# One ReLU of the next pair placed ahead of the next block's exponential on ScalarE (two adaLN layers: RWKV with experts, then pairwise attention with a ternary feed-forward)

## The chip, the core and the metric

The kernel runs on one core of a Trainium2 chip. A core has four compute engines that take their instructions in order, each from its own queue: TensorE (PE in the profile; its weight loads are listed as PEld), VectorE (DVE), ScalarE (ACT) and GpSimd (POOL). SyncE (SP) issues transfers. Engines wait for each other through semaphores. The metric is the device time of one launch in microseconds: the median of several runs, without a profiler.

## The reference

Two layers act on x of 4 batches x 1024 tokens x 256 channels, in float32. Each has an attention branch and a feed-forward branch, both behind a layer norm that is scaled and shifted per batch, and both added to x through a gate per channel. The first layer is an RWKV recurrence and a mixture of 8 experts. The second layer, where the change acts, has pairwise attention and a ternary feed-forward:

```python
q = einsum('bnc,ac->bna', X, Wq)            # a = 64
k = einsum('bnc,ac->bna', X, Wk)
Vy = einsum('bnc,dc->bnd', X, Wy_w) + Wy_b
e = relu(signed_sqrt(q[:, :, None, :] + k[:, None, :, :]))   # sqrt(relu(x)+1e-8) - sqrt(relu(-x)+1e-8)
scores = einsum('bija,a->bij', e, Wphi)
ex = exp(scores - max_j scores)
part1 = einsum('bij,bjc->bic', ex, Vy)
Ew = einsum('bij,bija->bia', ex, e)
part2 = einsum('bia,ca->bic', Ew, We_w) + We_b * denom
(part1 + part2) / (denom + 1e-9)

h = silu(x @ w1 * s1) * (x @ w2 * s2)       # 256 -> 1024
h = gelu(h @ h1 * s3); h = gelu(h @ h2 * s4)
y = h @ w3 * s5                             # 1024 -> 256
```

The array e has 4 x 1024 x 1024 x 64 elements, 268 million. Each one takes an add, a ReLU, a square root, a part in the scores and a part in Ew.

## The kernel before

The program runs the first layer in `first_layer`, up to about 1230 us, but leaves the experts of its last batch over. Then `pair_attention` (line 829 on) runs the second layer, with the left-over experts as the first task beside it, to about 4930 us. The last feed-forward tasks follow.

**Blocks, pairs, halves.** The queries are cut into 128 blocks of 32, 32 blocks to a batch. A block's work on e has 16 halves. Half i holds 16 queries x 8 channels on the 128 partitions and the 1024 keys along the free dimension: 16 queries by `i // 8`, the channel group by `i % 8`. Two halves make a pair, so a block has pairs p = 0 to 7; a pair lives in one slot, a tile of 128 x 2 x 1024, of a ring of 14 slots (`RING`).

**What is done to a half.** `kB[i % 8]` holds the keys of one channel group, repeated over the queries. One instruction adds the half's query (one number per partition) and takes the maximum with zero. Which engine does this is fixed by i: GpSimd for `ADD_ON_POOL` = 1, 3, 5, 9, 11, 13 (line 1387), ScalarE, as a ReLU with a bias, for `RELU_ON_SCALAR` = 2, 6, 8, 12, 14 (line 1409), VectorE for 0, 4, 7, 10, 15 (line 1398). ScalarE then takes the square root of the whole pair (line 1410), and TensorE multiplies it by the weights of the scores into the PSUM tile `sc` (line 1414, eight matmuls per pair).

**The softmax.** When all eight pairs are in, `top` takes the maximum over the keys on VectorE (lines 1424 and 1426) and brings the quarters together on TensorE (1427). `exps` forms `neg`, the negative maximum (VectorE, 1431), and the exponential (ScalarE, 1433). Behind the exponential, `switch` issues a SiLU or GELU of the feed-forward task if one is queued (1363). The square root, the exponential and the GELU or SiLU each have another activation table, so `ACT_TABLE_LOAD` instructions stand between them.

**The second use of e.** `spread` copies the exponentials to all partitions with matmuls against `pick` (`xb`, line 1440); `weigh` multiplies a half by `xb` in place and sums over the keys into a column of `ew` (VectorE, line 1460). `turn` and `turned` transpose the exponentials (1447, 1451). Every fourth block `finish` makes the attention's output from them: copies of `ew` (1480), matmuls into `o` (1511, 1523), the division (1530 to 1533) and the addition to x on GpSimd (1535). Every eighth block a feed-forward task `dense` of 256 tokens is added: matmuls at 1251, 1321 and 1342, their scaling on VectorE at 1286, 1305 and 1352.

**The order.** The scheduler leaves the order as it is written (`manual_schedule`); the loop at the end of `pair_attention` writes it. For block n it goes through p = 0 to 7. Each step weighs both halves of pair p of block n (with VectorE's adds for the next pair to be made between the two), puts in pieces of the tasks (`work`, with a budget per step, `ROOM`), and then begins and makes one pair of a later block:

```python
while begun <= 8 * n + p + ahead[0]:
    begin()
    make()
```

`begin` takes a slot and issues GpSimd's adds of a new pair; `make` runs `pair` (VectorE's adds if not yet done, ScalarE's ReLUs, the square root, the score matmuls) for the pair that was begun two calls earlier (`LEAD`). `ahead` is 13 while the left-over experts run, about the first 12 blocks, and 14 from then on. At p = 5 the loop calls `top` of block n + 1, at p = 6 `exps` and the first `spread` of block n + 1. With `ahead` = 14, pair 1 of block n + 2 has been made just before that exponential, and pairs 2 and 3 have been begun but not made.

**Slots.** A pair's slot comes free when its second half has been weighed. Which free slot a new pair gets is settled by the order in which the program first writes to the new tiles.

Of the kernel before, what the change touches and what calls it, by code (L numbers as in the profile page):

```python
# [8 lines left out]
AF = mybir.ActivationFunctionType  # L9
# [35 lines left out]
def block_kernel(ctx: ExitStack, tc: tile.TileContext, a, out):  # L45
# [26 lines left out]
    nc.gpsimd.memset(seen, 0.0)  # L72
    first_layer(tc, a, link, cols, seen, ident, eps)
    pair_attention(tc, a, link, out, cols, seen, ident, eps)


# [753 lines left out]
def pair_attention(tc, a, link, out, cols_of, seen, ident, eps):  # L830
# [10 lines left out]
    nc = tc.nc  # L841
    NB = T // 32
# [3 lines left out]
    with tc.tile_pool(name="at_k", bufs=1) as pk, tc.tile_pool(name="at_w", bufs=1) as wp, tc.tile_pool(  # L846
# [14 lines left out]
        kB, qtab, kds, vds = {0: {}}, {0: link["qt"][0]}, {0: link["kd"]}, {0: link["vd"]}  # L861
# [17 lines left out]
        for i in range(2):  # L879
            t = wp.tile([P, 4, P], F32, tag=f"ewt{i}", name=f"ewt{i}")  # L880
            nc.gpsimd.memset(t, 0.0)
            ewt.append(t)
            t = wp.tile([P, 4, 64], F32, tag=f"ew{i}", name=f"ew{i}")
# [379 lines left out]
        def follower():  # L1263

            return groups.get(stream[1]) if len(stream) > 1 else None
# [103 lines left out]
        class Block:  # L1369


            def __init__(self, n):
                self.n, self.b, self.s, self.added = n, n // NB, {}, set()
                self.sc = psc.tile([P, 512], F32, tag="sc", name="sc")

            def on_scalar(self, i):
# [5 lines left out]
            def begin(self, p):  # L1382
                self.s[p] = ring.tile([P, 2, T], F32, tag="s", name="s")
                for h in range(2):
                    i = 2 * p + h
                    if self.n and i in ADD_ON_POOL:
                        nc.gpsimd.tensor_scalar(  # L1387
                            self.s[p][:, h, :], kB[self.b][i % 8], self.query(i), 0.0, ALU.add, ALU.max
                        )

            def adds(self, p):
# [3 lines left out]
                for h in range(2):  # L1395
                    i = 2 * p + h
                    if not (self.n and i in ADD_ON_POOL or self.on_scalar(i)):
                        nc.vector.tensor_scalar(  # L1398
                            self.s[p][:, h, :], kB[self.b][i % 8], self.query(i), 0.0, ALU.add, ALU.max
                        )  # L1400

            def pair(self, p):
                t = self.s[p]
                s = p // 4
                self.adds(p)
                for h in range(2):
                    i = 2 * p + h
                    if self.on_scalar(i):
                        nc.scalar.activation(t[:, h, :], kB[self.b][i % 8], AF.Relu, bias=self.query(i))  # L1409
                nc.scalar.activation(t, t, AF.Sqrt, bias=eps_rho)  # L1410
                for h in range(2):
                    g = (2 * p + h) % 8
                    for j in range(4):
                        nc.tensor.matmul(  # L1414
                            self.sc[32 * j : 32 * j + 32, 0:256],
                            wsel[:, g, 16 * (1 - s) : 16 * (1 - s) + 32],
                            t[:, h, 256 * j : 256 * (j + 1)],
                            start=p == 0 and h == 0,
                            stop=p == 7 and h == 1,
                        )  # L1420
# [121 lines left out]
        N = B * NB  # L1542
        blocks = {0: Block(0)}
        begun = made = 0
# [3 lines left out]
        def work(room):  # L1548


            tick()
            turns[0] += 1
            if issues and turns[0] % 2:
                issues.pop(0)()
            for of in (tasks, stream):
                while of and room > 0:
                    got = next(of[0], self_done)
                    if got is self_done:
                        of.pop(0)
                    elif got is None:  # L1560
                        break
                    else:
                        room -= got
# [10 lines left out]
        def make():  # L1574
            nonlocal made
            n, p = made // 8, made % 8
            if n < N:
                blocks[n].pair(p)
                if n % NB == NB - 1 and n + 1 < N and p >= 4:
                    for g in range(2 * p - 8, 2 * p - 6):  # L1580
                        spread_keys(n // NB + 1, g)
            made += 1
# [13 lines left out]
        for n in range(N):  # L1596
            cur = blocks.pop(n)
            ew = ews[n // 4 % 2]
            if n % 4 == 0:
                exT = p2.tile([P, 4, 2, P], F32, tag="exT", name="exT")  # L1600
            nxt = n + 1 < N
            if n % NB == PREP and n // NB + 1 < B:
                stream.insert(min(1 + (follower() in heads), len(stream)), prepare(n // NB + 1))
            for p in range(8):
                if p == 0:
                    cur.spread(1)
                    cur.turn()
                if p == 2:
                    cur.turned(exT)
                cur.weigh(p, 0, ew)  # L1610
                if made < 8 * N:
                    blocks[made // 8].adds(made % 8)
                cur.weigh(p, 1, ew)
                if nxt and p == 5:
                    blocks[n + 1].top()
                if nxt and p == 6:
                    blocks[n + 1].exps()
                    blocks[n + 1].spread(0)
                work(ROOM[p])
# [3 lines that stand above are left out]
            if n % 4 == 3:  # L1623
                tasks.append(finish(n, ew, exT))
# [104 lines left out]
```

## Time and profile before

| | us |
|---|---|
| runs without a profiler | 5089.64, 5089.88, 5096.81; median 5089.88 |
| the profiled execution | 5104.67, its span 5102.4 |
| PE, DVE, ACT, POOL busy | 4335.7, 4171.3, 3691.2, 3401.3 |
| mean granted TensorE clock | 0.90 of full speed |

| row | count | mean ns |
|---|---|---|
| square root of a pair, L1410 | 1024 | 2000 |
| ReLU of a half on ScalarE, L1409 | 641 | 1138 |
| add of a half on VectorE, L1398 | 645 | 914 |
| add of a half on GpSimd, L1387 | 762 | 3798 |
| weighing of a half, L1460 | 2048 | 1210 |
| exponential, L1433 | 128 | 474 |
| its table load, L1433 | 128 | 1283 |

In a row of a group, the numbers after the count are the busy time in all, the mean of one in ns, and then the time for which the engine sat idle just before such instructions, with the line that ended most of it. In a row of a timeline the first two numbers are the start and the length in us, and square brackets give the idle time just before the instruction and what released it. Rows of a timeline can hold several instructions (x3). Times on GpSimd are rough.

### The profile page before, as it was taken

The page shows a single profiled execution, that of the slowest core. Times are in us where ns is not written, and L with a number is a line of the kernel's source. Part 1 is how long each engine was busy: PE and PEld are TensorE (multiplying, and loading weights), DVE is VectorE, ACT ScalarE, POOL GpSimd, SP SyncE. Part 2 cuts the span into 40 slices and gives each one's busy share as a digit, 9 for nine tenths or more (in the row PEclk, how much of TensorE's full clock was granted, in tenths as well). Part 3 has the DMA queues.
Part 4 walks back from the last instruction along what each step waited for, and adds up shares of the span by engine and source line. Part 5 has one row for each costly group of instructions (what it writes and reads, how often), then busy time and mean ns, then how long its engine had stood idle before and what let it go on. Part 6 is the DMA issues. An engine that isn't in the chain of part 4 may idle for free.

```text
span 5102.4 us, 75603 instructions
## 1 busy us (share of the span) xinstructions
PE 4335.7 (85%) x28714; PEld 2442.9 (48%) x28714; DVE 4171.3 (82%) x7255; ACT 3691.2 (72%) x3438; POOL 3401.3 (67%) x1231
## 2 busy tenths in 40 slices
PE   6788888878688879888897989888889889798888
PEld 2233333333344545555554555555455556455557
DVE  4877777776889888889888888888888988988871
ACT  2322322225888898999998989999888999999961
POOL 3433434334678778788877778787877877887840
PEclk7798988889788999999898999999889989999999
DMA  4333333343012222222121323222123322122223
GB/s 136 83 101 110 95 93 92 93 118 119 27 33 71 80 82 91 101 78 69 57 85 47 121 76 110 70 70 84 60 83 103 103 70 84 60 79 67 75 80 114
DMA packets 255946, 429.41 MB, mean 84 GB/s; under 512 B 71784, under 2 KB 142624, under 8 KB 255328
## 3 DMA queue, kind: packets, MB, share of 16 engines
q1 hardware_dynamic: 252512, 422.09, 26.5%
q8 instruction: 226, 3.70, 0.3%
q10 hardware_dynamic: 2880, 1.98, 0.1%
q14 instruction: 136, 1.11, 0.1%
q0 software_dynamic: 192, 0.52, 0.0%
HBM read 400.32 MB, written 40.93 MB: 86 GB/s over the span
## 4 chain that ended last, share of the span: by engine, by line
PE 35%; ACT 18%; DVE 15%; issue 7%; POOL 1%; DMA 0%; ACTq 0%; POOLq 0%; SPq 0%; DVEq 0%
PE ff_ps L1321 14%; PE sc L1414 10%; DVE s L1460 9%; ACT s L1410 9%; ACT s L1409 4%; PE xb L1440 3%; DVE s L1398 2%; PE out_ps L1342 2%; PE o L1511 2%; ACT L1410 2%; ACT L1363 1%; PE o L1523 1%; ACT wide L1363 1%; PE ff_ps L1251 1%; ACT ex L1433 1%
## 5 line engine op out<-in xcount | busy, mean ns | idle before, releaser
L1387 POOL TENSOR_SCALAR s<-kB,qt 128x1024 f32<-128x1024 f32 x762 | 2883.6, 3798 | 600.7 <-DVE ew L1460 476.4
L1460 DVE CUSTOM_DVE_ANT_0 s<-s,xb 128x1024 f32<-128x1024 f32 x2048 | 2418.3, 1210 | 36.2 <-PE xb L1440 35.0
L1410 ACT ACTIVATE s<-s,eps 128x2048 f32<-128x2048 f32 x1024 | 2027.2, 2000 | 76.1 <-DVE s L1398 29.8
L1414 PE MATMUL sc<-s,wsel 128*32 128x256 f32 x16384 | 1194.8, 416 | 398.9 <-ACT s L1410 396.8
L1321 PE MATMUL ff_ps<-wide,fw 128*128 128x256 f32 x4096 | 1007.5, 395 | 29.3 <-ACT wide L1363 25.7
L1414 PEld LDWEIGHTS sc<-s,wsel 128*32 128x32 f32 x16384 | 456.2, 115 | 997.7 <-ACT s L1410 590.1
L1321 PEld LDWEIGHTS ff_ps<-wide,fw 128*128 128x128 f32 x4096 | 766.9, 195 | 238.1 <-issue 99.4
L1409 ACT ACTIVATE s<-kB,qt 128x1024 f32<-128x1024 f32 x641 | 729.0, 1138 | 17.9 <-DVE acc L594 16.6
L1398 DVE TENSOR_SCALAR s<-kB,qt 128x1024 f32<-128x1024 f32 x645 | 588.9, 914 | 0.9 <-DMA same<-in_same_dram 0.9
L736 POOL TENSOR_TENSOR kv<-vb,out_k 128x512 f32<-128x512 f32 x256 | 324.1, 1274 | 279.1 <-DVE state L804 196.8
L611 PE MATMUL e_ps<-wd,hid 128*128 128x512 f32 x896 | 427.8, 625 | 0.4 <-DVE acc L594 0.4
L1440 PE MATMUL xb<-ex,pick 64*128 64x256 f32 x2048 | 328.8, 445 | 57.0 <-ACT ex L1433 57.0
L804 DVE TENSOR_TENSOR_SCAN state<-dec,carry,kv 128x512 f32<-128x512 f32 x256 | 325.9, 1273 | 10.8 <-ACT dec L791 10.7
L611 PEld LDWEIGHTS e_ps<-wd,hid 128*128 128x128 f32 x896 | 175.6, 202 | 249.0 <-issue 242.3
L1440 PEld LDWEIGHTS xb<-ex,pick 64*128 64x128 f32 x2048 | 197.7, 209 | 196.4 <-ACT ex L1433 97.7
L1251 PE MATMUL ff_ps<-wide,fw 128*128 128x256 f32 x1024 | 265.4, 408 | 6.1 <-ACT wide L935 5.8
L806 DVE TENSOR_TENSOR pr<-state,rec 128x512 f32<-128x512 f32 x256 | 176.0, 688 | 87.6 <-ACT state L802 34.4
L796 ACT COPY carry<-state 128x1 f32<-128x1 f32 x255 | 47.9, 188 | 269.6 <-DVE state L804 268.2
L1251 PEld LDWEIGHTS ff_ps<-wide,fw 128*128 128x128 f32 x1024 | 197.2, 201 | 65.3 <-issue 26.6
L1424 DVE TENSOR_REDUCE sc<-sc 128x1 f32<-128x256 f32 x128 | 54.9, 429 | 210.0 <-PE sc L1414 210.0
L1305 DVE TENSOR_TENSOR wide<-ff_ps,ffn_s 128x512 f32<-128x512 f32 x128 | 87.8, 686 | 168.0 <-PE ff_ps L1321 168.0
L1433 ACT ACTIVATE ex<-sc,neg 128x256 f32<-128x256 f32 x128 | 60.7, 474 | 199.9 <-DVE neg L1431 198.9
(252 smaller groups left out, 4006.6 us busy)
## 6 DMA issues: line engine op xcount, KB each, us to landing
fw<-in_ffw_dram SPq DMA_DIRECT2D x354, 512.0 KB
vb<-vd SPq DMA_DIRECT2D x1024, 64.0 KB
lent<-vd SPq DMA_DIRECT2D x64, 514.0 KB
wd<-in_w_down_dram SPq DMA_DIRECT2D x28, 1024.0 KB
kB<-kd SPq DMA_DIRECT2D x32, 512.0 KB
lent<-in_We_dram SPq DMA_DIRECT2D x32, 512.0 KB
kd<-nd SPq DMA_DIRECT2D x24, 512.0 KB
vd<-out_v SPq DMA_DIRECT2D x8, 512.0 KB
```

What stands on the lines that cost most here:

```text
L611: nc.tensor.matmul(ps, hid[:, k, t * P : (t + 1) * P], wd[:, k, :], start=k == 0, stop=k == HID // P - 1)
L736: nc.gpsimd.tensor_mul(kv, vb[:, g % 2, :], ready[u]["k"][:, n // HN, :])
L804: nc.vector.tensor_tensor_scan(s[:, 1 : U + 1], dec, kv, c, ALU.mult, ALU.add)
L1251: nc.tensor.matmul(ps[:, h, :], w[:, k, o : o + P], hT[:, k, :], start=k == 0, stop=k == 1)
L1321: nc.tensor.matmul(ps[:, h, :], w[:, k * P : (k + 1) * P], of[:, k, :], start=k == 0, stop=k == 7)
L1387: nc.gpsimd.tensor_scalar(self.s[p][:, h, :], kB[self.b][i % 8], self.query(i), 0.0, ALU.add, ALU.max)
L1398: nc.vector.tensor_scalar(self.s[p][:, h, :], kB[self.b][i % 8], self.query(i), 0.0, ALU.add, ALU.max)
L1409: nc.scalar.activation(t[:, h, :], kB[self.b][i % 8], AF.Relu, bias=self.query(i))
L1410: nc.scalar.activation(t, t, AF.Sqrt, bias=eps_rho)
L1414: nc.tensor.matmul(self.sc[32 * j : 32 * j + 32, 0:256], wsel[:, g, 16 * (1 - s) : 16 * (1 - s) + 32], t[:, h, 256 * j : 256 * (j + 1)], s ...
L1440: nc.tensor.matmul(xb[:, 256 * j : 256 * (j + 1)], pick[q, j % 2, s, :], self.ex[q, :], start=True, stop=True)
L1460: nc.vector.tensor_tensor_reduce(t[:, h, :], t[:, h, :], self.xb[s], 1.0, 0.0, ALU.mult, ALU.add, ew[:, self.n % 4, col : col + 1])
```

## The change

ScalarE's ReLUs of a pair get a function of their own, `relus`, which `pair` calls where the code stood before and which does nothing the second time. At p = 6 the loop calls it, ahead of `exps`, for the pairs that have been begun but not yet made.

```diff
             def __init__(self, n):
-                self.n, self.b, self.s, self.added = n, n // NB, {}, set()
+                self.n, self.b, self.s, self.added, self.relued = n, n // NB, {}, set(), set()
...
+            def relus(self, p):
+                if p in self.relued:
+                    return
+                self.relued.add(p)
+                for h in range(2):
+                    i = 2 * p + h
+                    if self.on_scalar(i):
+                        nc.scalar.activation(self.s[p][:, h, :], kB[self.b][i % 8], AF.Relu, bias=self.query(i))
+
             def pair(self, p):
                 t = self.s[p]
                 s = p // 4
                 self.adds(p)
-                for h in range(2):
-                    i = 2 * p + h
-                    if self.on_scalar(i):
-                        nc.scalar.activation(t[:, h, :], kB[self.b][i % 8], AF.Relu, bias=self.query(i))
+                self.relus(p)
                 nc.scalar.activation(t, t, AF.Sqrt, bias=eps_rho)
...
                 if nxt and p == 6:
+                    for m in range(made, min(begun, 8 * N)):
+                        blocks[m // 8].relus(m % 8)
                     blocks[n + 1].exps()
                     blocks[n + 1].spread(0)
```

With `ahead` = 14 the pairs are 2 and 3 of block n + 2. Pair 2 (halves 4 and 5) has no half on ScalarE, pair 3 has half 6. With `ahead` = 13 they are pairs 1 and 2, and the half is number 2. So one ReLU of 128 x 1024 goes ahead of each of 126 of the 128 exponentials. On ScalarE it is moved past the exponential with its table load, the queued SiLU or GELU with its load, the load back to the square root's table, and, with `ahead` = 14, the square root of pair 2. The orders on the other engines' queues are unchanged, and no transfer is issued at another place. The slot of pair 3 is now first written at this ReLU, so pair 3 gets the slot of the current block's pair 5, where it had that of pair 6; pair 4, whose first write is GpSimd's add of half 9, gets the slot of pair 6 where it had that of pair 5.

## The prediction, made before the changed kernel was run

> **What bounds the kernel now.** I read the page's engine totals first, then its costliest groups, then the busy time of the pair-attention stage (1230 to 4930 us), where the change acts, and last the timelines of ScalarE, TensorE, VectorE and GpSimd over one stretch of eight blocks (4228 to 4455 us).
>
> ```profile
> PE 4335.7 (85%) x28714; PEld 2442.9 (48%) x28714; DVE 4171.3 (82%) x7255; ACT 3691.2 (72%) x3438; POOL 3401.3 (67%) x1231
> ```
>
> ```profile
> 1230.00:4930.00 3700.00, 3168.53 (x25276) 1915.49 (x25277) 3219.28 (x5739) 3337.77 (x2506) 2918.72 (x814) 0.91 0.23 75
> ```
>
> The columns of the second are window, length, then PE, PE loads, DVE, ACT, POOL. Over the whole run ScalarE looks idle for a quarter; inside the stage it is the fullest engine: 3337.8 of 3700 is 90%, beside 87% for VectorE and 86% for TensorE. It idles for 362 us there, and the groups say where:
>
> ```profile
> L1387 POOL TENSOR_SCALAR s<-kB,qt 128x1024 f32<-128x1024 f32 x762 | 2883.6, 3798 | 600.7 <-DVE ew L1460 476.4
> ...
> L1410 ACT ACTIVATE s<-s,eps 128x2048 f32<-128x2048 f32 x1024 | 2027.2, 2000 | 76.1 <-DVE s L1398 29.8
> ...
> L1409 ACT ACTIVATE s<-kB,qt 128x1024 f32<-128x1024 f32 x641 | 729.0, 1138 | 17.9 <-DVE acc L594 16.6
> L1398 DVE TENSOR_SCALAR s<-kB,qt 128x1024 f32<-128x1024 f32 x645 | 588.9, 914 | 0.9 <-DMA same<-in_same_dram 0.9
> ...
> L1424 DVE TENSOR_REDUCE sc<-sc 128x1 f32<-128x256 f32 x128 | 54.9, 429 | 210.0 <-PE sc L1414 210.0
> ...
> L1433 ACT ACTIVATE ex<-sc,neg 128x256 f32<-128x256 f32 x128 | 60.7, 474 | 199.9 <-DVE neg L1431 198.9
> ```
>
> 199 us of ScalarE's idle time lie ahead of the exponential, which waits for VectorE's maximum, which waits (210 us) for the last score matmuls. That is the pocket that the change puts a ReLU of 1.138 us into. But the pocket is uneven. Listing the idle time ahead of each of 127 exponentials: 53 have 1.13 us or more, 48 have under 0.05, the rest lie between. Cut off at 1.134 us each, the pockets hold 74.7 us: that is all that can be filled. In the other direction the exponentials become late by 127 x 1.134 - 74.7 = 69 us in sum. Neither sum is a time yet: what counts is which wait ends last next.
>
> Two exponentials, one with a pocket and one without:
>
> ```profile
> 4252.03 1.28 ACT L1433 ACT_TABLE_LOAD   x1
> 4257.26 0.47 ACT L1433 ACTIVATE ex<-sc,neg 128x256 f32<-128x256 f32 x1 [3.95 <-DVE neg L1431]
> 4257.75 1.28 ACT L1410 ACT_TABLE_LOAD   x1
> 4259.05 2.00 ACT L1410 ACTIVATE s<-s,eps 128x2048 f32<-128x2048 f32 x1
> 4260.95 1.13 ACT L1409 ACTIVATE s<-kB,qt 128x1024 f32<-128x1024 f32 x1
> ```
>
> ```profile
> 4424.31 0.47 ACT L1433 ACTIVATE ex<-sc,neg 128x256 f32<-128x256 f32 x1
> 4424.81 1.28 ACT L1363 ACT_TABLE_LOAD   x1
> 4426.10 2.00 ACT L1363 ACTIVATE wide<-wide 128x1024 f32<-128x1024 f32 x2
> 4428.12 1.28 ACT L1410 ACT_TABLE_LOAD   x1
> 4429.41 2.00 ACT L1410 ACTIVATE s<-s,eps 128x2048 f32<-128x2048 f32 x1
> 4431.32 1.13 ACT L1409 ACTIVATE s<-kB,qt 128x1024 f32<-128x1024 f32 x1
> ```
>
> In both, the last row is the ReLU that moves up, in front of the exponential's table load. In the first it costs nothing and ScalarE is 1.13 us ahead from then on; in the second the exponential, the GELU behind it and the next square root all come 1.13 us later.
>
> **The change part by part.** Nothing is added or removed. One ReLU (pair 3, half 6) per block moves past the exponential's load (1.28), the exponential (0.47), the stream's activation where there is one, the load back (1.28) and the square root of pair 2 (2.00). TensorE's, VectorE's, GpSimd's and SyncE's own orders stay; no DMA is issued at another place. The number of table loads stays too, since ReLU runs between two square roots today without one.
>
> *What the moved ReLU waits for.* Its slot must be free: it takes the slot of the current block's pair 5, whose last weighing is ahead of the maximum on VectorE, so this wait has ended before any exponential can run. At the three changes of batch it also waits for a load of `kB`, now ahead of an exponential: 3 times; bounds 0 and some 5 us in all (the group's whole wait on that load was 0.7 us), taken as 0.
>
> *ScalarE, over the eight blocks from 4228.6 to 4454.5*, a pattern that returns nine times (idle ahead of the exponentials 2.06, 3.95, 0.47, 0, 4.36, 0, 0, 0):
> 1. 4228.6, idle 2.06: hidden. The 1.13 us lead dies at the next exponential, which waits 3.95 us for TensorE's side. 0.
> 2. 4257.3, idle 3.95: hidden; the lead dies at a square root that waits 1.05 us for a VectorE add. 0.
> 3. 4283.6, idle 0.47: exponential and GELU 0.67 late; TensorE has a wait of 0.72 ahead where it regains this. 0.
> 4. 4313.0, no idle: 0.67 late (it starts with a lead of 0.47), but TensorE isn't waiting for it. 0.
> 5. 4342.5, idle 4.36: hidden, a lead of 1.13.
> 6. 4367.2, no idle: the lead pays for the ReLU, GELU on time. 0; the new lead dies at two waits for the stream's layer norm (0.47 and 1.18).
> 7. 4398.1, no idle: 1.13 late; TensorE and VectorE have made it up by 4413. 0.
> 8. 4424.3, no idle: 1.13 late, and this one lies on the path:
>
> ```profile
> 4431.47 1.07 PE L1414 MATMUL sc<-s,wsel 128*32 128x256 f32 x16 [2.65 <-ACT s L1410]
> ```
>
> ```profile
> 4441.74 0.87 DVE L1286 SCALAR_TENSOR_TENSOR wide<-ff_ps,ffn_s,wide 128x256 f32<-128x256 f32 x2 [3.24 <-PE ff_ps L1251]
> ```
>
> TensorE waits for that square root, then goes through the FFN matmuls that VectorE waits for, and the maximum at 4454.5 comes some 1.06 us later. Sum of a period: +1.06.
>
> *Slots.* The ring gives a slot to whoever writes it first in the program. The ReLU now takes pair 5's slot, so GpSimd's first add of pair 4 (half 9) must wait for pair 6's second weighing; in the trace it starts 1.7 to 7.1 us ahead of that weighing's end. GpSimd then starts the next adds up to 0.67 us later; it waits 476 us for VectorE in 204 places, and pair 4's square root comes some 8 us after that weighing with the add done at 3.9. Cost 0; without that cover it would be 0.67 per block.
>
> *VectorE beside GpSimd.* Some VectorE adds are stretched while GpSimd adds:
>
> ```profile
> 4339.63 1.60 DVE L1398 TENSOR_SCALAR s<-kB,qt 128x1024 f32<-128x1024 f32 x1
> ```
>
> ```profile
> 4329.63 11.05 POOL L1387 TENSOR_SCALAR s<-kB,qt 128x1024 f32<-128x1024 f32 x3
> ```
>
> ```profile
> 4436.63 0.74 DVE L1398 TENSOR_SCALAR s<-kB,qt 128x1024 f32<-128x1024 f32 x1
> ```
>
> The first add, 2.6 us into GpSimd's third operation, took 1.60 us; the last, 2.1 us into one too (GpSimd ran three from 4426.80), took 0.74. The stretched add sits directly ahead of the maximum of step 5, and GpSimd's half 9 would no longer be there: -0.85 per period. In exchange the add after the maximum (half 7) comes some 1.7 us into half 9. The Trainium skill ("SBUF — State Buffer", Who interferes with whom) says that where the two share a port pair, the second to issue blocks fully until the first ends. By that rule this add would stand for 3.9 - 1.9 = 2 us in each of 126 blocks, 252 us of VectorE's time, and with a third of it on the path +84 us. The row says otherwise: 0.74 under a running GpSimd add, and 1.60 at the worst. I go by the rows: 0.
>
> *Sum.* Nine periods: 9 x (1.06 - 0.85) = +2. Two of them leave by the GELU: 2 x 0.67 = +1.3. The opening blocks (idle 3.58, 1.01, 2.57, 1.01, 1.02, 2.57, 1.93, 1.01, with ScalarE otherwise full): up to 1 us each, half of it taken, -4. Three exponentials with a pocket of 1.20 to 1.31 and the chain running along ScalarE: -3. The two stretches in which the next batch's keys are prepared: -3 for the relieved adds, +1.4 for one late exponential in each. In all -5 us. Against the profiled execution (span 5102.4, 5104.67 with what lies around it) that is 5100; the unprofiled median is 5089.88, so 5085.
>
> **The rivals.**
> - *The pockets count* (23%): ScalarE is the fullest engine, and a lead of 1.13 us is kept in one of three places rather than dying at the next wait: -74.7 / 3 = -25, 5065. For it: 90% busy. Against it: five of the eight steps above. All kept would be 5015.
> - *The late exponential counts* (29%, slower): 48 exponentials have nothing to hide the ReLU; behind them wait the spread matmuls, GELUs and a square root that TensorE waits for. It decides once the square root of pair 2 comes late on TensorE's path in more than about 16 blocks (16 x 1.13 = 18, less the 8 gained elsewhere, is 10 us). With 24, or two of the eight in each period and some more: 27 - 8 = +19, 5109. For it: step 8. Against it: steps 3, 4 and 7, where another wait absorbs it.
> - *GpSimd becomes late or stretches VectorE elsewhere* (9%, slower): 0.2 us per block is 126 x 0.2 = +25, 5115; by the rule above far more.
> - *It doesn't do what it says*: the order of instructions shows the ReLU ahead of 126 of 128 exponentials, so this is out.
>
> **How the numbers follow.** My forecast, a wash, gets 39%. What a measurement of this kernel can tell from no change is about 0.2%, 10 us. A wash spreads 5075 to 5098 by itself: the path's +1.06 alone (without the relieved adds) gives +3, and all of the opening's gain -9. Of its 39 parts some 8 fall beyond -10 us and 3 beyond +10. Faster: 23 + 8 = 31. Slower: 29 + 9 + 3, less 4 for small ends of the late-exponential case, is 37. The rest, 32, is within 0.2%. The range leaves a tenth out at each end: 5058 to 5118.
>
> **What would show it.** Idle ahead of the exponential falls from 199 to about 125 us, while its start in step 8 is some 1.1 us later against its block; VectorE's add ahead of the maximum loses its 1.60s; GpSimd's wait for the weighing grows by some us per block; TensorE's wait for square roots (397 us) hardly moves. I'm wrong if TensorE's waits on ScalarE grow by tens of us, if VectorE's adds grow beyond 0.91 us in the mean, or if ScalarE's idle falls with the span.

## The result: a little slower, and where the time went

The changed kernel takes 5103.84 us, the median of 15 runs (5100.74 to 5112.10), against 5095.16 us for the kernel before (15 runs between them, 5088.85 to 5103.79). The ratio is 1.0019, with an interval of 1.0012 to 1.0027. The time lies inside the forecast range, but the forecast was 5 us faster, and the kernel is 9 us slower.

The engine totals of the profile after, whose execution took 5108.61 us with a span of 5106.4:

```profile
PE 4360.7 (85%) x28714; PEld 2464.8 (48%) x28714; DVE 4162.2 (82%) x7255; ACT 3686.8 (72%) x3438; POOL 3380.9 (66%) x1231
```

The same instructions as before (28714, 7255, 3438, 1231), with VectorE and GpSimd a little less busy, and TensorE 25 us busier. The pair-attention stage in one window (window, length, PE, PE loads, DVE, ACT, POOL, granted TensorE clock, DMA share, GB/s):

```profile
1230.00:4930.00 3700.00, 3189.90 (x25247) 1934.62 (x25248) 3206.24 (x5736) 3332.41 (x2506) 2898.90 (x814) 0.89 0.22 75
```

TensorE is busy for 3189.9 us where it was busy for 3168.5, with nearly the same rows in the window (25247 and 25276), at a granted clock of 0.89 where it was 0.91. The forecast gave no place to this. The groups that answer to those shown of before:

```profile
L1387 POOL TENSOR_SCALAR s<-kB,qt 128x1024 f32<-128x1024 f32 x762 | 2865.0, 3773 | 629.0 <-DVE neg L1437 342.9
...
L1416 ACT ACTIVATE s<-s,eps 128x2048 f32<-128x2048 f32 x1024 | 2017.7, 1998 | 96.1 <-DVE s L1398 52.6
L1420 PE MATMUL sc<-s,wsel 128*32 128x256 f32 x16384 | 1193.5, 417 | 348.7 <-ACT s L1416 347.6
...
L1398 DVE TENSOR_SCALAR s<-kB,qt 128x1024 f32<-128x1024 f32 x645 | 576.8, 895 | 0.2 <-DMA kB<-kd 0.2
...
L1446 PE MATMUL xb<-ex,pick 64*128 64x256 f32 x2048 | 329.2, 445 | 85.6 <-ACT ex L1439 85.6
```

```profile
L1439 ACT ACTIVATE ex<-sc,neg 128x256 f32<-128x256 f32 x128 | 60.7, 474 | 151.6 <-DVE neg L1437 150.6
```

(The exponential is line 1439 now, the square root 1416, the score matmuls 1420, the spread 1446.) ScalarE's idle time ahead of the exponential fell from 199 to 151 us, TensorE's wait for the square roots from 397 to 348, and its wait for the exponential rose from 57.0 to 85.6.

Set against each other, the two traces tell where the time went. A shift is the start of an instruction in the trace after, less its start before; a negative one is a lead. The first exponential of the loop comes 1.4 us earlier than before, the eleventh 11.3 us earlier: the opening gains 10 us. Between the fourteenth (-10.9) and the 127th (+3.4) the lead is lost and more: 14.4 us.

In the stretch of eight blocks that the forecast went through step by step, the shift of the exponential is -3.6 at step 1 and at step 6, -1.8 at step 7, -1.9 at step 8 and -0.5 at the next one. But an exponential with the moved ReLU ahead of it can come late on ScalarE while nothing else is late yet. How far a block has got is told better by the moment at which VectorE has the maximum that the exponential waits for (`neg`, line 1431 before and 1437 after). By this measure the shift is -3.6 at step 1, -3.3 at step 6, -2.8 at step 7 and -3.0 at step 8: most of the lead is still there. The 2.5 us go in step 8 alone. Its maximum and the next one, before and then after:

```profile
4423.51 0.16 DVE L1431 TENSOR_REDUCE neg<-sc 128x1 f32<-128x4 f32 x1
4454.32 0.15 DVE L1431 TENSOR_REDUCE neg<-sc 128x1 f32<-128x4 f32 x1
```

```profile
4420.53 0.16 DVE L1437 TENSOR_REDUCE neg<-sc 128x1 f32<-128x4 f32 x1
4453.85 0.16 DVE L1437 TENSOR_REDUCE neg<-sc 128x1 f32<-128x4 f32 x1
```

TensorE's rows in step 8. The wait of 2.65 us before stands in the prediction; behind it came

```profile
4432.47 2.01 PE L1511 MATMUL o<-lent,exT 128*128 128x257 f32 x8
```

and after, the wait and the same row behind it:

```profile
4429.53 1.67 PE L1420 MATMUL sc<-s,wsel 128*32 128x256 f32 x16 [3.58 <-ACT s L1416]
4431.12 3.05 PE L1517 MATMUL o<-lent,exT 128*128 128x257 f32 x8
```

The first row starts at a shift of -1.94, 1.04 us later than the lead of 2.98, which is what the late square root was forecast to cost. Then the two rows, which took 1.07 and 2.01 us before, take 1.67 and 3.05: 1.64 us more, for the same instructions. The granted clock (the number behind POOL's) over this place, before and then after:

```profile
4426.91:4430.32 3.41, 1.91 (x8) 1.35 (x8) 3.27 (x7) 3.38 (x4) 3.41 (x1) 1.00 0.58 226
4430.32:4433.74 3.42, 2.27 (x22) 1.55 (x23) 3.42 (x6) 3.39 (x3) 3.42 (x2) 1.00 0.00 0
```

```profile
4426.45:4429.86 3.41, 0.33 (x8) 0.25 (x12) 3.41 (x8) 3.40 (x3) 3.41 (x2) 1.00 0.00 0
4429.86:4433.27 3.41, 3.41 (x21) 2.03 (x14) 3.41 (x7) 3.32 (x3) 3.41 (x2) 0.50 0.00 0
```

The clock stays at 1.00 before and falls to 0.50 after. The stretch returns nine times. Over the nine, the maximum loses 15.3 us in step 8 and gains 2.2 us in steps 1 to 7 together. In five of them the clock falls at this place in both kernels, and step 8 costs 0.7 to 1.3 us, 1.1 on the mean. In the other four it falls in the changed kernel only, and step 8 costs 2.2 to 2.6 us, 2.4 on the mean.

**What the clock goes by.** The windows above are not chosen freely. In both traces each record of the granted clock, but for the first and the last, lasts a whole multiple of 3.413 us: the clock changes on a fixed grid. Taking the windows of this grid from 1230 to 4930 us in both traces together, the clock of the next window goes with the share of the window in which TensorE is busy (the ends of matmuls are modelled in the profile, so the shares are not exact):

| TensorE busy in the window | windows | clock in the next |
|---|---|---|
| at full clock, under 45% | 171 | half in 167 |
| at full clock, 45 to 50% | 20 | half in 13 |
| at full clock, over 50% | 1543 | half in 6 |
| at half clock, under 80% | 190 | full in 1 |
| at half clock, 80 to 95% | 81 | full in 37 |
| at half clock, over 95% | 163 | full in 150 |

The two windows before were busy for 56 and 66%, the window after for 10%. The length of the wait does not decide it. In another return of step 8 the changed kernel loses the clock with 2.33 us, which lay within one window; a later run (ReLU behind the exponential in blocks without a pocket) keeps it in this step with 3.39 us, which fell on two windows:

```profile
4200.48 1.31 PE L1420 MATMUL sc<-s,wsel 128*32 128x256 f32 x16 [2.33 <-ACT s L1416]
4201.72 3.40 PE L1517 MATMUL o<-lent,exT 128*128 128x257 f32 x8
```

```profile
4441.80 1.07 PE L1422 MATMUL sc<-s,wsel 128*32 128x256 f32 x16 [3.39 <-ACT s L1418]
4442.80 2.00 PE L1519 MATMUL o<-lent,exT 128*128 128x257 f32 x8
```

The Trainium skill ("TensorE: Matmul & The Clock Gate", Part 1: The HAM clock gate) has such a gate: the clock goes to one half after an idle window of about 3.4 us and back after a busy one, and the window runs freely, whenever the work starts. The grid of 3.413 us agrees with it. That the window must be idle does not agree: in the 186 windows that lost the clock the longest idle stretch was 2.0 us in the median. Where a wait falls on the grid differs from run to run. The run below in which only the opening has the change has later blocks as before; it keeps the clock in step 8 in five of nine returns where the kernel before keeps it in four, and not in the same ones. So one return of a pattern does not show what a wait costs.

**Step 6.** Here the clock differs too, but little comes of it. TensorE's rows and the clock, first before:

```profile
4370.94 1.99 PE L1342 MATMUL out_ps<-fw,wide 128*128 128x256 f32 x8 [1.49 <-ACT wide L1363]
4374.25 1.07 PE L1414 MATMUL sc<-s,wsel 128*32 128x256 f32 x16 [1.32 <-ACT s L1410]
```

```profile
4365.47:4368.88 3.41, 2.95 (x22) 1.52 (x24) 3.41 (x7) 3.36 (x4) 3.41 (x1) 0.50 0.00 0
```

and after:

```profile
4364.15 2.08 PE L1446 MATMUL xb<-ex,pick 64*128 64x256 f32 x8 [0.89 <-ACT ex L1439]
4367.37 3.78 PE L1342 MATMUL out_ps<-fw,wide 128*128 128x256 f32 x8 [1.14 <-ACT wide L1363]
4371.08 1.41 PE L1420 MATMUL sc<-s,wsel 128*32 128x256 f32 x16
```

```profile
4361.59:4365.01 3.42, 2.53 (x20) 1.17 (x14) 3.42 (x7) 3.37 (x4) 1.55 (x2) 0.50 0.00 0
4365.01:4368.42 3.41, 2.27 (x9) 1.28 (x8) 3.33 (x6) 3.38 (x3) 3.41 (x2) 0.50 0.00 0
```

In both kernels TensorE comes into this stretch at half clock. Before, a window busy for 87% is followed by full clock; after, the spread waits 0.89 us for the exponential, two windows are busy for 74 and 67%, and the clock stays at half. The eight feed-forward matmuls take 3.78 us in place of 1.99. But the kernel before then waits 1.32 us for a square root, and the changed one no longer has to. Most of the 1.79 us goes into that wait: TensorE's lead is 3.57 us at the start of the row, 3.17 at the next, which still starts at half clock, and 2.84 at the one behind it.

Summed between the fourteenth and the 127th exponential, TensorE was busy at half clock for 438 us before and for 521 us after.

### The profile page after: what moved, and what is told of

The parts are those of the page before. It is cut to its first block, busy times and chain, and to the rows that moved or that the text cites. A ratio compares the mean times of both kernels' runs of the same rounds, so it can differ in the third digit from the quotient of the medians.

```text
span 5106.4 us, 75611 instructions
## 1 busy us (share of the span) xinstructions
PE 4360.7 (85%) x28714; PEld 2464.8 (48%) x28714; DVE 4162.2 (82%) x7255; ACT 3686.8 (72%) x3438; POOL 3380.9 (66%) x1231
## 4 chain that ended last, share of the span: by engine, by line
PE 52%; ACT 22%; DVE 19%; issue 6%; DMA 1%; SPq 0%; POOL 0%; ACTq 0%; DVEq 0%; POOLq 0%
PE ff_ps L1321 16%; PE sc L1420 11%; ACT s L1416 10%; PE e_ps L611 6%; DVE s L1466 5%; ACT s L1409 4%; PE xb L1446 3%; DVE state L804 2%; PE out_ps L1342 2%; PE o L1517 2%; DVE s L1398 2%; DVE pr L806 2%; PE ff_ps L1251 1%; ACT L1439 1%; ACT wide L1363 1%
## 5 line engine op out<-in xcount | busy, mean ns | idle before, releaser
L1409 ACT ACTIVATE s<-kB,qt 128x1024 f32<-128x1024 f32 x641 | 729.0, 1138 | 17.9 <-DMA kB<-kd 17.1
L1398 DVE TENSOR_SCALAR s<-kB,qt 128x1024 f32<-128x1024 f32 x645 | 576.8, 895 | 0.2 <-DMA kB<-kd 0.2
L1446 PE MATMUL xb<-ex,pick 64*128 64x256 f32 x2048 | 329.2, 445 | 85.6 <-ACT ex L1439 85.6
```

What stands on the lines that cost most here:

```text
L1398: nc.vector.tensor_scalar(self.s[p][:, h, :], kB[self.b][i % 8], self.query(i), 0.0, ALU.add, ALU.max)
L1409: nc.scalar.activation(self.s[p][:, h, :], kB[self.b][i % 8], AF.Relu, bias=self.query(i))
L1446: nc.tensor.matmul(xb[:, 256 * j : 256 * (j + 1)], pick[q, j % 2, s, :], self.ex[q, :], start=True, stop=True)
```

## The experiments

Ratios are to the kernel before, run on the same chip in the same rounds; behind each is its 95% interval. Theory E: the ReLU in front delays what comes behind it where there is no pocket, and the opening gains. Theory S: the swapped slots cost. Theories C and H: the granted clock. Theory L: only lateness counts, not the clock.

| run | median, us | ratio | interval |
|---|---|---|---|
| changed kernel | 5103.84 | 1.0019 | 1.0012 to 1.0027 |
| opening only | 5091.02 | 0.9985 | 0.9975 to 0.9995 |
| later blocks only | 5119.82 | 1.0041 | 1.0029 to 1.0054 |
| slots swapped, ReLU not moved | 5095.87 | 0.9995 | 0.9986 to 1.0004 |
| ReLU behind every exponential | 5159.09 | 1.0120 | 1.0106 to 1.0134 |
| opening and pockets | 5080.50 | 0.9968 | 0.9955 to 0.9980 |
| blocks without a pocket only | 5123.84 | 1.0059 | 1.0045 to 1.0073 |
| the same, behind the exponential | 5124.00 | 1.0057 | 1.0044 to 1.0069 |
| blocks with a pocket only, behind it | 5104.33 | 1.0014 | 1.0005 to 1.0023 |
| before, waits filled | 5087.49 | 0.9989 | 0.9980 to 0.9998 |
| changed kernel, waits filled | 5083.21 | 0.9979 | 0.9970 to 0.9988 |
| opening and pockets, waits filled | 5063.56 | 0.9939 | 0.9926 to 0.9951 |
| pair 2 ahead of the exponential | 5095.89 | 1.0002 | 0.9993 to 1.0011 |
| without a pocket, waits filled | 5109.66 | 1.0017 | 1.0008 to 1.0025 |
| the same, behind it, waits filled | 5112.01 | 1.0019 | 1.0010 to 1.0028 |

**The two halves of the change.** In the second run `n < 13` is `n >= 13`.

```diff
-                    for m in range(made, min(begun, 8 * N)):
+                    for m in range(made, min(begun, 8 * N) if n < 13 else made):
```

> The moved ReLU only for the first 13 blocks of the loop (n below 13); afterwards as before. Theory E (late exponential): the opening keeps a gain of some 10 us, and later blocks, where the exponential has no idle time ahead of it, lose more than that. Then this run is about 10 us faster than before: ratio 0.998, near 5085. Theory S (the loss comes from the swapped slots, GpSimd's half 9 starting later): also about 0.998, since the slots are swapped only in the opening. Theory C (the loss is a lower granted TensorE clock, 0.892 in the profile after against 0.900 before): the time follows the clock, and the ratio is near 1.002 if the clock is 0.892 again.

> The moved ReLU only from block 13 of the loop on. Theory E: the losses without the opening's gain, some 15 to 20 us slower than before, ratio 1.003 to 1.004. Theory S: the same. Theory C: near 1.002 like the changed kernel, no more. If the two halves of the change don't add up to the changed kernel's 1.002, something carries over from the opening.

The opening alone is 0.9985, the later blocks alone 1.0041. Their effects, -0.15% and +0.41%, add up to +0.26% beside the +0.19% of the whole, within the intervals. In the traces the opening alone goes from -3.2 us at the first exponential to -13.1 at the eleventh (10 us), and the later blocks alone from -2.0 at the fourteenth to +19.4 at the 127th (21 us). The opening's profile had a clock of 0.904, that of the later blocks 0.890. A clock that merely happened to be low in one execution is out: the loss comes with the later blocks.

**The slots.**

```diff
+                    for m in range(made, min(begun, 8 * N)):
+                        blocks[m // 8].claim(m % 8)   # VectorE: s[p][:, h, 0:1] = 0 for halves on ScalarE
                     blocks[n + 1].exps()
```

> ReLUs where they were before; a VectorE write of one column per partition (overwritten by the ReLU) claims the slot of pair 3 ahead of the exponential, so the slots are swapped as in the changed kernel. The write adds some 0.07 us of VectorE per block ahead of the maximum, 126 times, of which a third counts: up to 3 us. Theory E: ratio 0.999 to 1.001 (the relieved VectorE adds may even win some us). Theory S: 1.002 to 1.004, as the changed kernel's later blocks.

0.9995: the swapped slots cost nothing that can be seen. VectorE's adds fell to a mean of 873 ns from 914 without a clear gain in time. Theory S is out, and the relief of VectorE's adds is worth 3 us by this run's median, and 7 at the most by its interval.

**The exponential or the square root behind it.**

```diff
                     blocks[n + 1].exps()
+                    for m in range(made, min(begun, 8 * N)):
+                        blocks[m // 8].relus(m % 8)
```

> The ReLU goes between the exponential (with the queued SiLU or GELU) and the square root of pair 2: it passes only that square root. The exponential is on time, the square root behind it is 1.13 us late in every block. Theory E: the opening's gain is lost (pockets stay empty), and the later blocks' loss is lost too as far as it comes from the exponential and the GELU; what comes from the late square root stays. I expect 0.999 to 1.002. If it is 1.003 or more, it is the late square root that costs, not the late exponential. Theory S: slots swapped or not decides, not this place.

The expectation was missed by far: 1.0120. With the exponential on time everywhere and only pair 2's square root 1.13 us late, the kernel loses six times as much as the change. So the late exponential is not needed for a loss.

**By pockets.** The blocks after the opening are taken by the idle time that their exponential had in the profile before: 48 with 1.0 us or more, 46 under 0.05. Each kernel has the condition of one of these lists; two of them have the ReLU behind the exponential, as in the last diff.

```diff
+POCKET = [14, 15, 23, 25, 26, 29, 30, 33, ...]
+BARE = [18, 19, 20, 21, 27, 28, 32, 34, ...]
-                    for m in range(made, min(begun, 8 * N)):
+                    for m in range(made, min(begun, 8 * N) if n in BARE else made):   # or n < 13 or n in POCKET
```

> The moved ReLU in the opening (n below 13) and, later, only ahead of the 48 exponentials that had 1.0 us or more of idle time in the profile before. Theory E (leads from pockets die at the next wait; only exponentials without a pocket lose): as the opening alone, 0.9985, within 0.001. Theory P (filled pockets are worth something in the later blocks): below 0.9975. If it is above 1.000, exponentials with a pocket lose too, and the division by pockets is wrong.

> The moved ReLU, after the opening, only ahead of the 46 exponentials that had under 0.05 us of idle time. Theory E: nearly all of the 21 us that the later blocks lost, 1.003 to 1.0045. If it is under 1.001, the loss comes from blocks with a pocket.

> In the same 46 blocks, the ReLU goes behind the exponential (and its SiLU or GELU) and ahead of pair 2's square root. That square root is as late as in the run with the ReLU ahead of the exponential, the exponential is on time. If the late exponential costs, this run is at 1.000 to 1.0015; if the late square root costs, it is as slow as the other, 1.003 to 1.0045; in between, both.

> In the 48 blocks with a pocket (none in the opening), the ReLU goes behind the exponential: the pocket stays empty and pair 2's square root is 1.13 us late where it starts at once after the exponential's load. With the ReLU behind the exponential everywhere the kernel was 1.012, 58 us of it from the second exponential on. If those 58 us come from the pocket blocks, where TensorE waits for ScalarE right after an exponential that was itself the last to come, this run is at 1.006 to 1.009; if from the others, at 1.000 to 1.003.

The pockets seem to be worth something: 0.9968 with them, 0.9985 without, so some 8 us for 48 blocks. The two intervals just overlap (0.9975 to 0.9980); between the fourteenth and the 127th exponential the two traces differ by 6.8 us in the same direction. The blocks without a pocket cost 28 us, more than expected, and it makes no difference whether the ReLU stands ahead of the exponential or behind it. What both places have in common is the late square root of pair 2, which TensorE waits for in step 8. Its mark on the clock shows over all runs: the row of TensorE behind that wait ran at full clock in four of nine returns in the kernel before and in five, two, three and three in the runs that leave this square root on time (opening only, slots swapped, opening and pockets, pockets behind it). It did so in none of nine in the changed kernel, with the later blocks only, with the blocks without a pocket only, and with the ReLU behind every exponential; behind the exponential of the blocks without a pocket it was four.

The 28 us are not spread evenly over the 46 blocks. In the trace with the ReLU ahead of the exponential the nine steps 8 lose 15.6 us, as in the changed kernel, and the nine steps 6 lose 9.7 us, where they lose 1.0 in the changed kernel. In six of the nine, step 6 is one of the 46 blocks, and its exponential comes 1.0 us late against its maximum: the ReLU moved in step 5, into a pocket, gave the lead that paid for this in the changed kernel, and here it stays where it was.

The last of the four came out in the lower of its two cases, 1.0014. The 1.0120 of the ReLU behind every exponential is more than these two parts (0.57% and 0.14%) give together; the 19 blocks between the lists, or an effect of one block on the next, must hold the rest, and this was not split further.

In the run with the ReLU behind the 46 exponentials TensorE isn't busy at half clock longer than before, 442 us beside 438. But part of that time lies elsewhere. Its rows at the feed-forward task of step 6:

```profile
4377.78 2.84 PE L1344 MATMUL out_ps<-fw,wide 128*128 128x256 f32 x8 [2.09 <-ACT wide L1365]
4382.14 1.93 PE L1422 MATMUL sc<-s,wsel 128*32 128x256 f32 x16 [1.51 <-ACT s L1418]
4384.00 3.63 PE L1344 MATMUL out_ps<-fw,wide 128*128 128x256 f32 x12
```

Against 1.99, 1.07 and 2.86 us before, these three are 2.48 us longer, and the nine steps 6 of this run lose 14.6 us by the maximum. The sum of time at half clock is not the measure, then; where it lies is.

**The clock, taken away.** In places where a kernel's own profile has TensorE waiting for over 1.0 us ahead of a pair's score matmuls or of a spread, small matmuls are put in front, so many that about half a microsecond of the wait should stay. They add zeros to the scores of a block.

```diff
+            def fill(self, count, first):
+                for _ in range(count):
+                    nc.tensor.matmul(self.sc[0:16, 0:P], wsel[:, 0, 0:16], ident, start=first, stop=first)
...
+                blocks[n].fill(FILL_PAIR.get(made, 0), p == 0)
                 blocks[n].pair(p)
...
+                    if n + 2 < N:
+                        blocks[n + 2].fill(FILL_SPREAD.get(n + 1, 0), False)
                     blocks[n + 1].spread(0)
```

> The kernel before, with small matmuls (16 rows of zero weights x 128, added as zeros to the scores of a block) put in the places where TensorE waited over 1.0 us for ScalarE in its own profile, so many that about half a microsecond of the wait stays: 790 in 135 places. Theory H (TensorE's granted clock falls to 0.5 behind a long wait and its next matmuls run at half speed): TensorE is busy for 438 us at half clock in the later blocks; the fill takes some of that away and the kernel gets faster, 0.985 to 0.998. Theory L (only lateness counts, the clock is not on the path): 1.000 to 1.003, the fill costs or does nothing.

> The changed kernel with the same kind of fill in the places where its own profile has such waits: 791 matmuls in 133 places. Theory H: the changed kernel loses in its later blocks because it is busy for 521 us at half clock, 83 more than before; with the fill its loss against the filled kernel before goes, and the opening's gain is left: it is faster than the filled kernel before by some 5 to 10 us. Theory L: it stays 8 to 10 us slower than the filled kernel before.

> The kernel with the moved ReLU in the opening and ahead of the 48 exponentials with a pocket (0.9968 without fill), with the fill for its own waits: 786 matmuls in 142 places. Theory H: as much faster than unfilled as the kernel before is, and so the fastest of all. Theory L: 0.997 to 1.000.

The stage of the filled changed kernel, as one window:

```profile
1230.00:4930.00 3700.00, 3266.88 (x26953) 2049.14 (x26951) 3220.06 (x5771) 3332.68 (x2508) 2900.62 (x813) 0.94 0.23 76
```

The clock is 0.94 in place of 0.89 (it is 0.94 in the filled kernel before too). Over the whole run TensorE does 1582 rows more, and the kernel is 20.6 us faster than without them; the kernel before gains 6.5 us, less than the 0.985 to 0.998 that I had expected if the clock counts, and more than nothing. The changed kernel now stands 4 us below the filled kernel before (5083.21 and 5087.49), where it stood 9 us above; their intervals overlap, so "no longer slower" is what is shown.

Between the fourteenth and the 127th exponential the changed kernel lost 14.4 us on the kernel before; filled, it loses 6.3, and from the 63rd on nothing (-0.2 there, -2.2 at the 127th). By the maximum, the nine steps 8 cost 0.4 us in place of 15.3, but the nine steps 7 now lose 6.0 us where they gained 3.1. So something like half of the later blocks' loss goes with the fill. What is left need not be lateness alone: filled, TensorE is still busy at half clock for 270 us, beside 258 in the filled kernel before, and the two fills are not the same. The opening-and-pockets version is the fastest of all with the fill, 0.9939.

**The square root earlier.** In the 46 blocks without a pocket pair 2 is made ahead of the exponential; ReLUs stay where they were.

```diff
+                    if n in BARE:
+                        make()
                     blocks[n + 1].exps()
...
                     begin()
-                    make()
+                    if made < begun - LEAD:
+                        make()
```

> The ReLUs stay where they were before. In the 46 blocks without a pocket the whole of pair 2 (VectorE's add, square root, its score matmuls) is made ahead of the exponential, so the square root is 2 us earlier or more, and the exponential 2.0 us later. Two runs with that square root 1.13 us late and the exponential late or on time were equally slow (1.0059 and 1.0057). If the square root's place is what counts, this one is faster than before: 0.994 to 0.999. If a late exponential costs, it is slower: 1.002 to 1.010.

1.0002: neither of the two. An earlier square root is not worth what a later one costs, or the later exponential takes it away; the run doesn't tell which.

**How much of the loss without a pocket goes with the fill.**

> The moved ReLU ahead of the 46 exponentials without a pocket only (1.0059 without fill), with the fill for its own waits: 799 matmuls in 122 places. Theory H: this kernel is busy at half clock for 518 us in the later blocks, 80 to 87 more than before; with the fill it comes within 5 to 15 us of the filled kernel before (0.9989): 1.000 to 1.002. Theory L: the 28 us stay, 1.004 to 1.006.

> The ReLU behind the same 46 exponentials (1.0057 without fill), with the fill for its own waits: 855 matmuls in 139 places. Without fill this kernel is busy at half clock no longer than before (442 us), so theory H alone doesn't explain its 28 us: if they come from the late square root itself (TensorE's wait ahead of pair 2 and what is queued behind it), they stay, 1.003 to 1.005, while the run with the ReLU ahead of the exponential falls. If both fall alike, the fill does something else than I think.

Both fall alike, from 1.0059 to 1.0017 and from 1.0057 to 1.0019. Against the filled kernel before (0.9989) that leaves 0.28% and 0.30%, half of what they lost without the fill. For the second I had expected the loss to stay, from the unchanged sum of half-clock time; the rows above show why the sum misled.

## Why the prediction was wrong, by its steps

Shifts are those of the maximum unless the exponential is named. The forecast's terms for the later blocks add up to about -1.4 us; in the traces they come to +14.4.

- *Step 8, +1.06.* This is the term that failed: the wait was right, its price too small. TensorE came to the row behind the wait 1.04 us later, as forecast. But the forecast let the matmuls behind it run as fast as before; the clock fell, they took 1.64 us longer, and the next maximum came 2.5 us later. Over the nine returns step 8 costs 1.7 us each, 15.3 in all where 9.5 was forecast: 1.1 us where the clock fell in both kernels, which is the forecast's own figure, and 2.4 in the four returns in which it fell only after the change.
- *VectorE's adds, -0.85 per period.* The row came as forecast:

```profile
4336.58 0.75 DVE L1398 TENSOR_SCALAR s<-kB,qt 128x1024 f32<-128x1024 f32 x1
```

  This is the add that took 1.60 us, and the mean fell from 914 to 895 ns. The adds behind the maximum were not blocked as the weighed rule would have it (its sum takes 1.9 us where the text beside it has 1.7; with 1.7 it would be 2.2 us a block); in either trace an add takes 1.91 us at the most. In five of the nine returns the maximum of step 5 comes 0.8 to 0.9 us earlier against that of step 4. But in each of them 0.65 us or more is lost again by step 6, so that the 9 x 0.85 that the sum set against step 8 was not there. My reading, which no run tests: the exponential of step 6 follows ScalarE's own work without idle time in both kernels, so an earlier maximum moves nothing there.
- *Opening, -4 us forecast.* Right in sign, mis-sized: 10 us in the trace, 7.6 by the medians. I had counted half of each pocket; nearly all of about 1 us each was kept.
- *Steps 1 to 5, 0.* Right: the exponential's shift is -3.6 at step 1 and at step 6. The late exponential of step 4 (0.9 us later, 0.67 forecast) was made up at step 5.
- *Steps 6 and 7, 0.* Right in the sum: the shift is -3.3 at step 6 and -3.0 at step 8, and the exponential of step 7, 1.0 us late against its maximum, is made up before step 8, as forecast. Over the nine returns the two steps gain 2 us. In part this is luck, since the forecast did not see that the feed-forward matmuls would run at half clock for lack of a window that is busy enough; the wait behind them took most of it.
- *The pockets' leads die.* Mostly: 48 pockets bring about 8 us, hardly clear of the noise. The idle time ahead of the exponentials fell by 48 us and not by 74.7. In the eight blocks it falls from 2.06 to 1.01 us at step 1 and from 4.36 to 3.32 at step 5, but at step 2, right behind step 1, it does not (3.95, then 4.08): between these two exponentials ScalarE has as many ReLUs as before.
- *Slots and GpSimd, 0.* Right (0.9995; GpSimd's idle time ahead of its adds is 629 us in all, 601 before).
- *The wait for keys at a change of batch, 0.* Right: the ReLUs' idle time is 17.9 us before and after.
- *The rivals.* The late-exponential one came nearest: it forecast 19 us slower, 9 were measured. It also named the right thing, a square root of pair 2 that comes late on TensorE's path. But it asked for more than 16 such blocks at 1.13 us each. In the changed kernel nine, at 1.7 us each, make up the loss.
- *The signs.* TensorE's wait for the square roots, which was to hardly move, fell from 397 to 348 us, and the wait ahead of the spread grew by 29. Taken together these two waits are 20 us shorter in the slower kernel, so the sign that I had named, TensorE's waits for ScalarE growing by tens of us, would not have told it. The idle time ahead of the exponentials was to fall to about 125 us and fell to 151.

## What to carry to other kernels

A wait of TensorE has a second price that its length doesn't show: whether it leaves a window of the clock so little busy that the matmuls behind it run at half speed. In these traces a window is 3.41 us, the limit lies near 45% busy on the way down and between 80 and 95% on the way up, and where the windows fall differs from run to run. So before moving work by a microsecond, read the granted clock of the rows behind each wait of TensorE on the path, over all returns of a pattern and not in one.

And when a piece of work is moved ahead of another, measure the shift where the work that others wait for is ready. The moved piece makes its neighbour late by itself, and that alone costs nothing yet: here by 1.0 us in step 7, all of it made up.

## What was not expected of the hardware

That zeros can pay: 790 small matmuls more made the kernel before 0.11% faster, and 791 made the changed one 0.40% faster (5083.21 against 5103.84), with the granted clock of the whole profile going from 0.900 to 0.929 and from 0.892 to 0.927. And that a wait of 2.33 us can lose the clock where one of 3.39 us keeps it, where what tells is the busy share of a fixed window.
